# Last image's spectral filter: tokens stored twice side by side, one full-width first product instead of two half-width ones

## The chip, the cores and the metric

The kernel runs on one core of one Trainium2 chip, in one launch. A core has a matrix engine (TensorE, PE in the profile; its loads of the stationary operand are listed apart as PEld), VectorE (DVE), ScalarE (ACT), GpSimd (POOL), and a sync engine (SP), which here issues DMA transfers. The metric is device time in microseconds (us), before and after measured in alternation; less is better.

## The reference

Four images of 64x64 tokens with 96 channels pass through four layers. Layer 0 is a group norm with a selective scan in four directions, layer 1 a 3x3 convolution, layer 2 linear attention and a quantised feed-forward net. The change is in layer 3, which filters each hidden channel over all 4096 tokens in frequency:

```
t = t + filter(layer_norm(t)); t = t + ffn(layer_norm(t))

def filter(x):                                  # x: (B, 4096, 96)
    h = relu(bn1(einsum('bnc,hc->bnh', x, w1)))     # 192 hidden channels
    X = fft(h, axis=1, norm='ortho')                # over the tokens
    xr = relu(X.real * rd - X.imag * idg + rb)
    xi = relu(X.imag * rd + X.real * idg + ib)
    y = ifft(xr + 1j * xi, axis=1, norm='ortho').real
    return bn2(einsum('bnh,ch->bnc', y, w2))
```

`rd` and `idg` are the diagonals of two 192x192 matrices; bn1 and bn2 are normalisations with stored statistics.

## The kernel before

**Staging.** Images are b = 0 to 3. Channels lie on partitions and tokens along the free axis: `t` is 96 x 4096 f32, cut in 8 blocks (NBLK) of 512 tokens (BLK), each of 8 image rows (RPB). For most of the run VectorE, GpSimd and ScalarE do the scans of layer 0, and everything else is fed in as side lanes: generators that yield pieces with a price for each engine, and are advanced when a budget allows. What follows the scans of images 0 to 2 goes that way. The last image's has nothing to run beside; it is `tail`, which calls `rest(..., deep=2)` with 8 PSUM banks and two or four buffers where other images have one, and is drained one piece of each live stream in turn. The order on each engine is thus fixed when the program is built; each engine runs its own queue in that order.

**The last image's stages.** `rest` yields lists of streams. One list holds the convolution of layer 1 (products `p_l`, L953), the layer norm of the attention, the attention, the feed-forward net and two more layer norms; the last of these has the result name `ln_s` and feeds the filter. At the head of that list's set-up two tiles get a row of ones behind their 96 channels, so that a product with 97 rows adds a bias: `ln` (L1420) and `turned` (L1425), each by one GpSimd memset of 1x4096. In time this set-up stands in the feed-forward net of image 2 (`p_f`, L1166 and L1186; `y` and `z`, L877 to L890; `t`, L1196).

**The layer norm `ln_s`** (from L964) works in two halves of four blocks. Per block: the mean is taken off by a product (`p_mean`, L997), VectorE copies the result to `ln` (L988), ScalarE squares it (`sq`, L989), a product sums the squares (`p_var`, L979). Per half ScalarE and VectorE form 1/sqrt(variance) (L1018 to L1029), and a product spreads it over the channels (`p_rstd`, L1049). `scale` (L1033 on) multiplies: VectorE reads `ln` and `p_rstd` and writes into `turned` (L1040). `turned` is 97 x 4096 in the order (n2, n1), where token = 64 n1 + n2, so this write goes with a stride of 64 elements. ScalarE's queue has at this place also the shift of `t` (L1381).

**The filter.** The transform over 4096 points is done as 64 x 64. `filter_in` (L1208) makes three streams `third(hc)`, one for each 64 hidden channels. Each has eight banks k of eight columns j; for the column n2 = 8k+j it computes h for 64 tokens (n1) by a product with `turned[:, n2, :]` (97 x 64) stationary and `w1s[:, hs]` (97 x 64, bn1 folded in) moving:

```
for at in (0, N1):                                             # L1239
    nc.tensor.matmul(
        p[at : at + N1, j, :], lhsT=ln3[:, 8 * k + j, :], rhs=w1s[:, hs],
```

It does so twice, to partitions 0 to 63 and 64 to 127 of the PSUM bank `p_h`, for the gate (VectorE, L1224) takes max(p_h, 0) times `filt`, which holds `rd` on the first 64 partitions and `idg` on the others, and writes `hb`; after bank 0 the biases are added as an impulse (`imp`, L893). Then come eight banks of `p_dft` (L1262): each of 64 channels' `hb` (128 x 64, stationary) against the 64-point table for real and imaginary part (128 x 64 moving each), 16 products a bank, evacuated to `z` by ScalarE and VectorE in turn (L877, L881) and stored by SP (L1274). A stream starts its products when the one before has issued all its p_h and, with deep = 2, `hb` and `z` have a buffer free, so the streams overlap by a bank.

`filter_mid` then loads `zl` and the table `tw`, does the second transform (`p_dft2a` L1319, `p_dft2b` L1328), the relus and `p_o` with w2 (L1302, L1303); `filter_turn` (`p_idft`, L1368) and `filter_out` (`p_idft`, L1407) do the inverse transform; a last layer norm and feed-forward net end the program. `filter_out` leaves by VectorE (L1394).

An f32 product leaves two load records and two matmul records in the trace.

Of the kernel before, what the change touches and what calls it, by code (L numbers as in the profile page):

```python
# [10 lines left out]
F32 = mybir.dt.float32  # L11
# [9 lines left out]
L = HW * HW  # L21
C = 96
# [6 lines left out]
RPB = BLK // HW  # L29
HID = 384  # L30
N1 = 64
# [42 lines left out]
def layers(ctx: ExitStack, tc: tile.TileContext, a: dict, out):  # L74
# [4 lines left out]
    nc = tc.nc  # L79
# [132 lines left out]
    def settle(held):  # L212


        while held:
            cost, f, args, since = held[0]
            if cost[1]:
                while ordered[0] and clock[0] == since and (clock[0] - 1) % 8 in (7, 0, 1):
                    yield NEXT
            yield cost  # L220
            held.pop(0)
            f(*args)

    def until(ready):
        while not ready():
            yield NEXT
# [641 lines left out]
    def blk(i):  # L868
        return slice(i * BLK, (i + 1) * BLK)
# [25 lines left out]
    def rest(b, take, deep, x1t=None, held=None):  # L895
# [6 lines left out]
        def count(stage):  # L902
            return ready.get(stage, 0)
# [60 lines left out]
        def layernorm(wk, hold, dst, source, result, previous=None):  # L964

            def half_of(h):
                half = range(h * NBLK // 2, (h + 1) * NBLK // 2)
                yield from until(lambda: count(source) > half[-1 if source == "t1" else 0])  # L970
                yield from until(lambda: h == 0 or (result, "var", 0) in ready or deep > 1)
                pv, give_v = yield from take("p_var", 128)
                held, squares = [], []

                def variance():

                    i, sq = squares.pop(0)
                    at = 32 * (i - half[0])
                    nc.tensor.matmul(pv[at : at + 32, :], lhsT=mean_w, rhs=sq, start=True, stop=True)  # L979

                def centred(i, pm, give):
                    if squares and deep == 1:
                        variance()
                    sq = wk.tile([C, BLK], F32, tag=f"sq{h}", name="sq", bufs=1 if deep == 1 else 4)
                    if ordered[0]:
                        nc.scalar.copy(hold[:, blk(i)], pm)
                    else:
                        nc.vector.tensor_copy(hold[:, blk(i)], pm)  # L988
                    nc.scalar.activation(sq, pm, AF.Square)  # L989
                    give()  # L990
                    squares.append((i, sq))

                for i in half:
                    yield from until(lambda: count(source) > i)
                    pm, give = yield from take("p_mean", C, held=held)
                    yield (0.9, 0, 0, 0)
                    nc.tensor.matmul(pm, lhsT=centre, rhs=t[:, blk(i)], start=True, stop=True)  # L997
                    if squares and deep == 1:
                        yield (0.9, 0, 0, 0)
                        variance()  # L1000
                    yield from settle(held)
                    held.append(((0, 1.25, 0, 0), centred, (i, pm, give), clock[0]))
                while held or squares:
                    yield NEXT
                    if deep > 1:
                        yield from settle(held)
                    while squares:
                        yield (0.9, 0, 0, 0)
                        variance()
                    yield from settle(held)  # L1010


                yield from until(lambda: h == 0 or count(result) >= NBLK // 2)
                yield from until(lambda: previous is None or count(previous) == NBLK)
                y, w = (wk.tile([128, BLK], F32, tag=k, name=k, bufs=deep) for k in ("rs_y", "rs_w"))
                yield NEXT
                yield (0, 1.9, 0, 0)
                nc.scalar.activation(y, pv, AF.Ln, bias=num[:, 2:3])  # L1018
                nc.scalar.activation(y, y, AF.Exp, scale=-0.5)
                nc.scalar.activation(w, y, AF.Square)  # L1020
                yield NEXT
                yield (0, 0, 0, 0.7)
                nc.vector.scalar_tensor_tensor(w, pv, 1e-5, w, ALU.add, ALU.mult)
                give_v(True)
                ready[result, "var", h] = True
                yield NEXT
                yield (0, 0.65, 1.3, 0)
                nc.scalar.activation(w, w, AF.Identity, scale=-0.5, bias=num[:, 3:4])
                (nc.gpsimd if ordered[0] else nc.vector).tensor_tensor(y, y, w, ALU.mult)  # L1029
                yield NEXT  # L1030
                yield NEXT

                def scale(i, pr, give):  # L1033
                    kept = {} if dst.dtype == F32 else {"saturate": False}
                    to, x = dst[:, blk(i)], hold[:, blk(i)]
                    if result == "ln_s" and deep > 1:
                        to = turned[:C, :].rearrange("p (n2 n1) -> p n1 n2", n1=N1)
                        to = to[:, i * RPB : (i + 1) * RPB, :]
                        x, pr = (v.rearrange("p (n m) -> p n m", m=N1) for v in (x, pr))
                    nc.vector.tensor_tensor(to, x, pr, ALU.mult, **kept)  # L1040
                    give(True)
                    ready[result] = i + 1

                held = []
                for i in half:
                    pr, give = yield from take("p_rstd", C, held=held)
                    yield (1, 0, 0, 0)
                    at = slice(32 * (i - half[0]), 32 * (i - half[0]) + 32)
                    nc.tensor.matmul(pr, lhsT=pick[at, :], rhs=y[at, :], start=True, stop=True)  # L1049
                    yield from settle(held)  # L1050
                    held.append(((0, 0, 0, 0.7), scale, (i, pr, give), clock[0]))
                yield NEXT
                yield from settle(held)

            return [half_of(0), half_of(1)]
# [152 lines left out]
        def filter_in(wk, ln):  # L1208

            if deep > 1:  # L1210
                ln3 = turned.rearrange("p (n2 n1) -> p n2 n1", n1=N1)
            else:
                ln3 = ln.rearrange("p (n1 n2) -> p n2 n1", n2=N1)

            def third(hc):
                hs = slice(hc * N1, (hc + 1) * N1)
# [16 lines left out]
                for k in range(8):  # L1233
                    p, give = yield from take("p_h", 128, held=held)
                    p = p.rearrange("p (n h) -> p n h", h=N1)
                    for j in range(8):
                        if j % 4 == 0:
                            yield (1.3, 0, 0, 0)
                        for at in (0, N1):  # L1239
                            nc.tensor.matmul(  # L1240
                                p[at : at + N1, j, :], lhsT=ln3[:, 8 * k + j, :], rhs=w1s[:, hs],
                                start=True, stop=True,
                            )
                    yield from settle(held)
                    held.append(((0, 0, 0, 0.7), gate, (k, p, give), clock[0]))
# [9 lines left out]
                for k in range(8):  # L1255
                    p, give = yield from take("p_dft1", 128, held=held)
                    p = p.rearrange("p (h k) -> p h k", k=N1)
                    for j in range(8):
                        if j % 4 == 0:
                            yield (1.3, 0, 0, 0)  # L1260
                        for ri in range(2):
                            nc.tensor.matmul(  # L1262
                                p[ri * N1 : (ri + 1) * N1, j, :], lhsT=hb[:, 8 * k + j, :],
                                rhs=dft1[:, ri, :], start=True, stop=True,
# [13 lines left out]
            if deep > 1:  # L1278
                return [third(hc) for hc in range(3)]
            return [chain(*(third(hc) for hc in range(3)))]  # L1280

        def filter_mid(wk, os_):
# [135 lines left out]
        wk = normal.sbuf(f"ln{b}")  # L1418
        ln = wk.tile([C + 1, L], F32, tag="ln", name="ln")
        nc.gpsimd.memset(ln[C : C + 1, :], 1.0)  # L1420
        turned = None
        if deep > 1:

            turned = wk.tile([C + 1, L], F32, tag="turned", name="turned")
            nc.gpsimd.memset(turned[C : C + 1, :], 1.0)  # L1425
        mid = Region(tc)
        wk = mid.sbuf(f"mid{b}")
# [8 lines left out]
        ], [mid] + ([held] if held else [])  # L1436
        inner = Region(tc)
        yield filter_in(inner.sbuf(f"filter_in{b}"), ln), [inner, normal]
        wide, inner = Region(tc), Region(tc)
        os_ = wide.sbuf(f"os{b}").tile([128, C, N1], F32, tag="os", name="os")  # L1440
# [11 lines left out]
        wk = last.sbuf(f"last{b}")  # L1452
# [77 lines left out]
    while len(delta_places) <= N:  # L1530
        p = delta_places[-1]
# [208 lines left out]
    wk = weights.sbuf("weights", side="right")  # L1740
# [45 lines left out]
    wk = head.sbuf("pre0")  # L1786
# [14 lines left out]
    with tc.manual_schedule():  # L1801
        ordered[0] = True
        pas = [decay(0, 0, True), None, None, None]
        for n in range(N + 1):
# [51 lines left out]
            for k, q in enumerate(reversed(range(NCH))):  # L1856
# [26 lines left out]
                to = dls[n, 0] if alone else pas[q]  # L1883
# [153 lines left out]
```

## Time and profile before

| quantity | us |
|---|---|
| three runs, median | 5797.89 |
| three runs, lowest and highest | 5784.04, 5817.91 |
| profiled execution, its device time | 5791.5 |
| profiled execution, span of the core | 5789.7 |
| last image after the scans, `ln_s` to the end of the third p_dft | 5568 to 5638.8 |
| of that, first p_h to the last p_dft | 5587.70 to 5638.8 |
| busy over the span: TensorE, VectorE, GpSimd, ScalarE | 4187.2, 4858.5, 4417.0, 3020.1 |
| memset of the ones row of `turned` (L1425) | 3.51, at 5396.62 |
| VectorE into `turned` (L1040), each of 8 | 1.016 |

Times in the trace run from the span's start. A row of the timeline or of the groups gives the engine and line, the operation, out<-in by the program's names, the shape (for TensorE partitions*stationary columns, then the moving operand), the type and the number of records; what stands in brackets or behind the last bar is the time that the engine had been idle and what ended it. Shares over the whole span mix the scans with the last image's stages; the last image's filter is read from its own stretch. The mean granted TensorE clock of the run is 0.771 of full speed; in single windows it is 0.50 or 1.00.

### The profile page before, as it was taken

Reading aid. Unit: us, or ns where it says so; the run is one execution under the profiler, and the core shown is the slowest. Engines: PE = TensorE matmul, PEld = TensorE weight load, DVE = VectorE, ACT = ScalarE, POOL = GpSimd, SP = SyncE. Lnnn points to the kernel's source line nnn. Section 1 sums busy time; section 2 is a strip of 40 time slices with the busy share of each in tenths; the row PEclk is TensorE's granted clock in tenths of the full one; section 3 lists DMA queues with packets and bytes.
Section 4 is the critical chain, followed back from the end, with each engine's and each line's share of the span. In section 5 each row is a group of like instructions: output and inputs, shape, how many; then the busy total and the mean of one; then the engine's idle time right before and its main releaser. Section 6 shows DMA issues by size and latency. Waiting matters only on the chain. (4 is left out here: it accounts for less than half of the span.)

```text
span 5789.7 us, 65093 instructions
## 1 busy us (share of the span) xinstructions
PE 4187.2 (72%) x19818; PEld 1630.1 (28%) x19818; DVE 4858.5 (84%) x3610; ACT 3020.1 (52%) x4188; POOL 4417.0 (76%) x2148
## 2 busy tenths in 40 slices
PE   8978887778864777664477776667778667667878
PEld 4422222222211221241331221334222114323345
DVE  4188988888899898999799999999999999978364
ACT  4767766766663356545454446444544544434233
POOL 1378887888898778888788989888898898867200
PEclk9888898888866876666777886678678666777888
DMA  4378878876699878788988868679887678886013
GB/s 123 111 212 229 233 200 235 233 204 196 195 252 236 225 206 222 207 240 244 255 235 224 228 182 222 197 210 248 235 235 202 171 207 237 251 227 183 20 43 101
DMA packets 470107, 1174.80 MB, mean 203 GB/s; under 512 B 90768, under 2 KB 155900, under 8 KB 469628
## 3 DMA queue, kind: packets, MB, share of 16 engines
q1 hardware_dynamic: 469756, 1170.64, 74.1%
q8 instruction: 157, 2.57, 0.2%
q14 instruction: 194, 1.59, 0.1%
HBM read 1013.53 MB, written 156.76 MB: 202 GB/s over the span
## 5 line engine op out<-in xcount | busy, mean ns | idle before, releaser
L1574 POOL TENSOR_TENSOR S<-S,rep 128x1024 f32<-128x1024 f32 x768 | 1807.2, 2356 | 546.2 <-DVE S L1894 495.1
L1587 ACT ACTIVATE pa<-dl,nega 128x1024 f32<-128x1024 f32 x1152 | 1285.3, 1117 | 1431.9 <-DVE S L1894 1072.3
L1570 POOL TENSOR_TENSOR B<-B,rep 128x1024 f32<-128x1024 f32 x768 | 1798.0, 2355 | 119.0 <-DMA B<-du_s 70.8
L1833 DVE TENSOR_TENSOR_SCAN S<-pa,S,B 128x1024 f32<-128x1024 f32 x576 | 1352.3, 2348 | 315.6 <-ACT pa L1587 133.5
L1601 PE MATMUL py<-S,red 128*32 128x512 f32 x3072 | 908.5, 848 | 755.1 <-POOL S L1574 503.6
L1884 DVE TENSOR_TENSOR_SCAN pa<-pa,edge,B 128x1024 f32<-128x1024 f32 x438 | 1029.7, 2351 | 55.5 <-ACT pa L1587 55.5
L1894 DVE TENSOR_TENSOR S<-S,pa 128x1024 f32<-128x1024 f32 x630 | 763.6, 1212 | 1.9
L1833 DVE TENSOR_TENSOR_SCAN S<-pa,B 128x1024 f32<-128x1024 f32 x192 | 436.4, 2273 | 44.8 <-ACT pa L1587 35.8
L1601 PEld LDWEIGHTS py<-S,red 128*32 128x32 f32 x3072 | 110.0, 125 | 1232.7 <-POOL S L1574 728.3
L402 PE MATMUL p_conv<-low,conv_w 128*96 128x512 f32 x864 | 437.4, 658 | 14.1 <-ACT u L414 9.6
L1884 DVE TENSOR_TENSOR_SCAN pa<-pa,B 128x1024 f32<-128x1024 f32 x192 | 440.8, 2296 | 5.3
L154 ACT COPY side<-side 96x256 f32<-96x256 f32 (+1 forms) x448 | 279.0, 629 | 187.7 <-DMA deltaT_s<-side 79.9
L1884 DVE TENSOR_TENSOR_SCAN dl<-pa,edge,B 128x1024 f32<-128x1024 f32 x138 | 323.1, 2341 | 20.6 <-ACT pa L1587 16.6
L1175 POOL CAST h<-y 128x1536 fp8e5<-128x1536 f16 x64 | 95.5, 1492 | 303.2 <-ACT y L886 281.9
L1579 POOL TENSOR_TENSOR dl<-dl,rep 128x1024 f32<-128x1024 f32 x138 | 325.6, 2360 | 0.1
L402 PE MATMUL p_conv<-high,conv_w 64*96 64x512 f32 (+1 forms) x576 | 269.7, 605 | 0.0
L997 PE MATMUL p_mean<-t,centre 96*96 96x512 f32 x256 | 173.7, 791 | 99.0 <-ACT sq L989 48.4
L402 PEld LDWEIGHTS p_conv<-low,conv_w 128*96 128x96 f32 x864 | 149.5, 181 | 319.0 <-issue 289.8
L1601 PE MATMUL py<-dl,red 128*32 128x512 f32 x552 | 220.2, 717 | 21.1 <-POOL dl L1579 21.1
L1609 ACT COPY ys<-py 128x512 f32<-128x512 f32 x384 | 221.8, 578 | 19.5 <-PE py L1601 18.3
L647 PE MATMUL p_y<-side,ident 96*96 96x512 f32 x336 | 210.0, 774 | 28.1 <-DVE side L681 8.6
L953 PE MATMUL p_l<-x,taps 96*96 96x504 f32 (+3 forms) x432 | 199.4, 613 | 16.2 <-DMA x<-x 12.7
(245 smaller groups left out, 6024.0 us busy)
## 6 DMA issues: line engine op xcount, KB each, us to landing
dl<-delta_s SPq DMA_DIRECT2D x768, 256.0 KB
B<-du_s SPq DMA_DIRECT2D x768, 256.0 KB
B<-duT_s SPq DMA_DIRECT2D x768, 256.0 KB
dl<-deltaT_s SPq DMA_DIRECT2D x768, 256.0 KB
z_s<-z SPq DMA_DIRECT2D x48, 512.0 KB
zl<-z_s SPq DMA_DIRECT2D x64, 384.0 KB
side<-y_s SPq DMA_DIRECT2D x120, 192.0 KB
rep<-bc_s SPq DMA_DIRECT2D x64, 256.0 KB
```

Source lines behind the costliest of these rows:

```text
L154: nc.scalar.copy(o.rearrange("p (w h) -> p w h", h=HW), t[:n, :].rearrange("p (h w) -> p w h", w=HW)[:, q * w : (q + 1) * w, :],)
L402: nc.tensor.matmul(p, lhsT=conv_w[: src.shape[0], k, oc * C : (oc + 1) * C], rhs=src[:, ky : ky + RPB, kx : kx + HW], start=(k == 0), stop ...
L647: nc.tensor.matmul(p, lhsT=ident[:C, :C], rhs=x, start=(j == 0), stop=(j == 2))
L1570: nc.gpsimd.tensor_tensor(Bs[n, q], Bs[n, q], reps[n // NG, 0, q], ALU.mult)
L1574: nc.gpsimd.tensor_tensor(Ss[n, q], Ss[n, q], reps[n // NG, 1, q], ALU.mult)
L1579: nc.gpsimd.tensor_tensor(dls[n, 0], dls[n, 0], reps[n // NG, 1, 0], ALU.mult)
L1587: nc.scalar.activation(pa, dls[n, q], AF.Exp, scale=nega[:, g : g + 1])
L1601: nc.tensor.matmul(py[32 * j : 32 * j + 32, :], lhsT=red, rhs=x[:, k * BLK : (k + 1) * BLK], start=(i == 0), stop=(i == len(terms) - 1),)
L1609: nc.scalar.copy(ys, pys.pop((n, half)))
L1833: nc.vector.tensor_tensor_scan(s, pas[q], Bs[n, q], Ss[n, q - 1][:, CH - 1 : CH] if q else 0.0, ALU.mult, ALU.add,)
L1884: nc.vector.tensor_tensor_scan(to[:, ::-1], pas[q][:, ::-1], Bs[n, q][:, ::-1], edge if k else 0.0, ALU.mult, ALU.add,)
L1894: nc.vector.tensor_tensor(Ss[n, q], Ss[n, q], to, ALU.add)
```

## The change

It applies only where `deep` is over 1, which is the last image. `turned` becomes 97 x 8192 in the order (n2, k, n1) with k = 0, 1: each column's 64 tokens stand twice side by side. VectorE writes the copy k = 0 as before, with a stride of 128 elements; a new ScalarE copy for each block (L1042 of the changed kernel) reads it and writes k = 1. The ones row is memset over 1x8192. The stationary operand of p_h is now 97 x 128, and one product writes all 128 partitions, so that the three streams have 192 products of p_h instead of 384. The values are the same. The lines after L1042 move down by two to five (gate L1224 to L1226, p_h L1240 to L1242, p_dft L1262 to L1266).

```diff
@@ -1034,10 +1034,12 @@
                     if result == "ln_s" and deep > 1:
-                        to = turned[:C, :].rearrange("p (n2 n1) -> p n1 n2", n1=N1)
-                        to = to[:, i * RPB : (i + 1) * RPB, :]
+                        both = turned[:C, :].rearrange("p (n2 k n1) -> p k n1 n2", k=2, n1=N1)
+                        to, again = (both[:, k, i * RPB : (i + 1) * RPB, :] for k in range(2))
                         x, pr = (v.rearrange("p (n m) -> p n m", m=N1) for v in (x, pr))
                     nc.vector.tensor_tensor(to, x, pr, ALU.mult, **kept)
+                    if result == "ln_s" and deep > 1:
+                        nc.scalar.copy(again, to)
                     give(True)
@@ -1208,7 +1210,7 @@
             if deep > 1:
-                ln3 = turned.rearrange("p (n2 n1) -> p n2 n1", n1=N1)
+                ln3 = turned.rearrange("p (n2 m) -> p n2 m", m=2 * N1)
@@ -1236,9 +1238,11 @@
-                        for at in (0, N1):
+                        for at in (0, N1) if turned is None else (0,):
                             nc.tensor.matmul(
-                                p[at : at + N1, j, :], lhsT=ln3[:, 8 * k + j, :], rhs=w1s[:, hs],
+                                p[at : at + N1, j, :] if turned is None else p[:, j, :],
+                                lhsT=ln3[:, 8 * k + j, :],
+                                rhs=w1s[:, hs],
                                 start=True, stop=True,
                             )
@@ -1421,7 +1425,8 @@
-            turned = wk.tile([C + 1, L], F32, tag="turned", name="turned")
+            turned = wk.tile([C + 1, 2 * L], F32, tag="turned", name="turned")
             nc.gpsimd.memset(turned[C : C + 1, :], 1.0)
```

In each engine's queue the order is otherwise kept. TensorE does the eight banks of p_h for hc 0 and one of hc 1, then p_dft for hc 0; seven banks of hc 1 and one of hc 2, then p_dft for hc 1; seven banks, then p_dft for hc 2. In ScalarE's queue the first four copies stand ahead of two L1381, each followed by a sq L989, and of the rstd chain of the second half, the last four ahead of the evacuations of p_dft.

## The prediction

> **What bounds the kernel now.** I read the core's line first (5789.7 us, mean granted TensorE clock 0.771), then the groups, shape by shape, for the stretch after the scans (5480 to 5790 us), because everything that the diff touches belongs to the last image's filter. In these rows out<-in is followed by partitions*columns of the stationary operand and the shape of the moving one.
>
> ```profile
> L1240 PE MATMUL p_h<-w1s,turned 97*64 97x64 f32 x768 | 26.1, 236 | 4.2 <-DVE turned L1040 3.6 <-issue 0.6
> L1302 PE MATMUL p_o<-w2a,ya 128*128 128x96 f32 x128 | 25.9, 284 | 0.0
> L1240 PEld LDWEIGHTS p_h<-w1s,turned 97*64 97x64 f32 x768 | 25.6, 151 | 6.0 <-DVE turned L1040 5.3 <-issue 0.7
> ...
> L1224 DVE SCALAR_TENSOR_TENSOR hb<-p_h,filt 128x512 f32<-128x512 f32 x24 | 23.0, 1061 | 3.3 <-PE p_h L1240 3.3
> ...
> L1407 PE MATMUL p_idft<-os,vs 128*96 128x64 f32 x128 | 11.1, 248 | 0.8 <-issue 0.8
> ```
>
> Then the timeline of that stretch, which says what ends each wait:
>
> ```profile
> 5584.05 3.60 DVE L1040 TENSOR_TENSOR turned<-ln,p_rstd 96x512 f32<-96x512 f32 x4 [2.17 <-PE p_rstd L1049]
> 5587.70 11.22 PE L1240 MATMUL p_h<-w1s,turned 97*64 97x64 f32 x282 [3.65 <-DVE turned L1040]
> ...
> 5599.26 7.68 PE L1262 MATMUL p_dft<-dft,hb 128*64 128x64 f32 x256 [0.34 <-DVE hb L1224]
> ...
> 5606.77 6.94 PE L1240 MATMUL p_h<-w1s,turned 97*64 97x64 f32 x231
> ...
> 5614.27 0.97 PE L1240 MATMUL p_h<-w1s,turned 97*64 97x64 f32 x25 [0.56 <-issue]
> 5615.24 7.68 PE L1262 MATMUL p_dft<-dft,hb 128*64 128x64 f32 x256
> ```
>
> From 5587.70 to the end of the third p_dft near 5638.8 TensorE is hardly ever idle: **51.0 us, bound by TensorE**, with the VectorE gate (0.94 to 0.95 us a bank, back to back) close behind. Of that, one bank of p_h is 32 records (every f32 product leaves two matmul and two load records). Warm, 231 records in 6.77 us are 29.3 ns a record, 0.94 us a bank: two records, one for each half of the columns, every 58.7 ns. Before the clock comes up a record costs 53.3, a bank 1.70.
>
> **What one full-width product costs** is not in the p_h rows. The nearest rows in shape are p_o (128 stationary columns) and L1407 (96), both one after the other:
>
> ```profile
> 5654.13 0.39 PE L1302 MATMUL p_o<-w2a,ya 128*128 128x96 f32 x2
> 5654.35 0.39 PE L1303 MATMUL p_o<-w2b,yb 128*128 128x96 f32 x2
> 5654.57 0.39 PE L1302 MATMUL p_o<-w2a,ya 128*128 128x96 f32 x2
> ...
> 5184.60 0.64 PE L1303 MATMUL p_o<-w2b,yb 128*128 128x96 f32 x2
> 5185.03 0.63 PE L1302 MATMUL p_o<-w2a,ya 128*128 128x96 f32 x2
> ...
> 5282.05 6.66 PE L1407 MATMUL p_idft<-os,vs 128*96 128x64 f32 x40
> ```
>
> Two p_o records take 0.22 us warm (111 each) and 0.43 cold (213 each); L1407 takes 85 warm (160 cold) with 64 moving columns and 96 stationary ones. L1407 moves the same 64 columns as p_h and p_dft, whose two tiles together take 58.7, and still needs 85; p_gram, with 97 stationary columns, 86. So the **stationary columns** set the pitch: about columns/1.2 + 5, which is 58 for 64, 85 for 96 and 112 for 128, and twice that cold.
>
> **The Trainium skill** agrees where it can be held against the trace. "TensorE: Matmul & The Clock Gate", section LDWEIGHTS: a load costs about its column count over 1.2, in ns, whatever the rows; that gives 107 and 80 against 111 and 85 seen, so loads and products overlap and the longer of the two, the load, sets the pitch. The same page, Part 3: tiles of the array work at once; the two p_h halves start 7 ns apart here. Its Part 1: half clock is the default, and a window of some 3.4 us with enough activity releases it. Here the window view gives
>
> ```profile
> 5283.10:5286.50 3.40, 3.40 (x24) 3.40 (x23) 3.40 (x3) 0.98 (x1) 3.40 (x3) 0.50 0.69 212
> ...
> 5590.00:5594.00 4.00, 4.00 (x85) 4.00 (x84) 2.97 (x4) 0.00 (x0) 0.00 (x0) 0.53 0.00 0
> 5594.00:5600.00 6.00, 5.66 (x192) 5.53 (x188) 4.95 (x6) 0.00 (x0) 0.00 (x0) 1.00 0.02 5
> ```
>
> (length; busy PE, PEld, VectorE, ScalarE, GpSimd; clock). The first row is wholly L1407, loads back to back, and the clock stayed at 0.50 after it; dense p_h brought full clock at 5593.74. The page also has N columns pass in N/2.4 ns warm, twice that cold; with the two passes of a record, moving columns flow for 107 of each 160 ns of L1407, 0.67, and all the time in dense p_h. I counted this share over all windows of the trace: of some 350 cold ones below 0.65 none was followed by a warm one, of those above 0.95 93%. "SBUF — State Buffer", section Who interferes with whom: a VectorE operation in a two-port mode is blocked until GpSimd's ends. The trace agrees:
>
> ```profile
> 5396.62 3.51 POOL L1425 MEMSET turned<- 1x4096 f32 x1
> ...
> 5396.72 3.56 DVE L890 TENSOR_SCALAR z<-z,b_L 96x512 f16<-96x512 f16 x1
> ...
> 5400.90 0.72 ACT L886 ACTIVATE y<-y,b_L 128x512 f16<-128x512 f16 x1 [2.60 <-DVE y L881]
> ```
>
> That L890 otherwise takes about 0.35 (5403.52).
>
> **The change, part by part** (against the profiled span).
> 1. *Memset of the ones row, 1x4096 to 1x8192.* One partition, so twice as long: 3.51 to 7.0. It blocks VectorE, and with it ScalarE, p_f and GpSimd's own L1196 behind it; the chain runs on to z L881 at 5411.60, for which p_l L953 waits, and TensorE is dense from there. **+3.5** (0 if another gap takes it, 3.6 at most). The wider tile costs no transfer.
> 2. *Eight ScalarE copies, 96x512.* The nearest row is L154, a strided copy of 96x256, median 627 ns. 512 elements by its slope give about **1.05 us** (0.6 if stride cost nothing, like the 0.57 to 0.60 of L989; 1.5 at most). VectorE's L1040 stays at 1016 ns (its stride doubles; up to 0.2 more each). The first four wait for L1040 and stand ahead of L1381 and sq L989 in ScalarE's queue. The last product of L1040 ends near 5573.87, so the copy ends near 5575.0, where sq started at 5574.43 before; p_var, the rstd chain and p_rstd follow: **+1.2** (0.5 to 2.5). Of the last four three run under L1040; the last follows it and p_h waits for it now: 1.05 plus a hand-over of 0.3, **+1.4** (0.65 to 3.1). The z copies behind them come much later.
> 3. *p_h: 768 records of 64 columns become 384 of 128.* Half the records at the pitch of p_o: 16 by 111.5 = **1.78 us a bank warm, 3.41 cold**, against 0.94 and 1.70. The gates hide below it. The order on TensorE keeps p_h of hc 0 and one bank of hc 1 ahead of the first p_dft, so nine banks come at once. Moving columns flow for 107 of 213 ns in the cold state, 0.50: no window like that released the clock, so I take all nine cold: 9 x 3.41 = 30.7. The first p_dft (0.95 dense) then brings the clock up after one to two windows: 5.1 us of it cold (96 records), the other 160 records at 29.3: 9.8. Eight banks warm 14.3, p_dft 7.55, seven banks 12.5, wait for the last gate 1.45, p_dft 7.55, five changes between full-width and half-width products at about 0.2 (what p_o to p_dft2a shows) 1.0: together 85 against 51.0, **+34**. At the head p_h has nothing behind it on TensorE that could run meanwhile. Behind it zl and tw are loaded and TensorE waits 10.09 us for them; the stores of z come later with p_dft, so nothing absorbs the loss.
>
> Sum: 3.5 + 2.6 + 34 = **+40 us**: span 5830, that profiled execution's 5791.5 to 5831.5. The median, 5797.89, lies 6.4 higher; with it **5837**.
>
> **Rivals.**
> - *It warms all the same.* If two windows of full-width product suffice, as with p_h before, 6 us of the nine banks are cold (1.8 banks) and 7.2 run at 1.78, 18.9 for 30.7, and the first p_dft saves 2.3: the part is 71, +20; sum +26, 5824. For it: the array is as full as in old p_h. Against: L1407 and cold p_o windows (5184.1, share 0.71) stayed cold.
> - *It falls back to half clock in hc 1 and hc 2 too.* Warm, the share is 53/111.5 = 0.48. Warm windows of 0.45 to 0.50 stayed warm 60% of the time, of 0.35 to 0.45 half. With one window warm in each, eight banks take 24.2, seven 20.8, each p_dft 9.8: 108 for the part, sum +63, 5861. L1407's 0.62 stays warm, and full-width windows of 0.45 to 0.48 mostly did, so I take the warm one.
> - *Not slower: the loads hide.* If the load of the next 128 columns ran wholly under the current product, a record would cost 53 to 58 ns, a bank 0.94 as the gates, and clock would come as before. Then only points 1 and 2 are left, +6, or about nothing if the memset is absorbed: 5798 to 5804. For it: half as many instructions, and no pairs to keep in step. Against: p_o, which runs at its load. It decides below about 94 ns a record warm, at which the sum is 29 us, 0.5%. A gain has no room: the gates would take over at 0.94.
> - *The change does nothing* can't be: one product per column block writes all partitions.
>
> **How the numbers follow.** Central case 0.48, warms early 0.14, falls back 0.22, loads hide 0.13, something else 0.03. I predict the first. The before runs spread by 0.3% either way, so a difference of medians carries some 12 us. Loads hidden and the low end of early warming make the low end, falling back the high end: 5806 to 5868 (the central case alone 5822 to 5852). About 0.5% (29 us) is what a measurement can tell from no change. The central case falls within it 1 time in 5, early warming 2 in 3, hidden loads nearly always: same 0.31, faster 0.02, slower 0.67.
>
> **What would show it.** Memset near 7.0 us with an L890 of the same length beside it; eight ScalarE copies near 1.05, and p_h starting 2 to 3 us later after the memset's delay is taken off; p_h records 213 ns apart in the first nine banks at clock 0.50, 111 apart after; gates waiting for p_h in every bank; the three p_dft at 7.6 but for the first, near 10. I am wrong if p_h records come 55 to 60 ns apart, if the clock rises inside the first nine banks, or if it falls in hc 1.

## The result and the profile after

The changed kernel takes 5856.09 us (median of 4 runs, 5846.63 to 5865.7) against 5793.13 for the kernel before, run in turn with it (5784.04 to 5817.91): a ratio of **1.0098, 95% interval 1.0079 to 1.0117**, slower by 46 to 68 us. The profiled execution has a span of 5856.7 us, 67.0 above the one shown of before.

The timeline of the last image's filter in the changed kernel (start, length, engine, line, operation; in brackets the idle time before it and what ended it), with the rows that answer to those of the prediction:

```profile
5579.80 2.75 DVE L1040 TENSOR_TENSOR turned<-ln,p_rstd 96x512 f32<-96x512 f32 x3
...
5580.85 3.64 ACT L1042 COPY turned<-turned 96x512 f32<-96x512 f32 x3 [0.15 <-DVE turned L1040]
...
5595.07 3.60 DVE L1040 TENSOR_TENSOR turned<-ln,p_rstd 96x512 f32<-96x512 f32 x4 [2.17 <-PE p_rstd L1051]
5596.12 4.77 ACT L1042 COPY turned<-turned 96x512 f32<-96x512 f32 x4 [3.94 <-DVE turned L1040]
5600.94 30.98 PE L1242 MATMUL p_h<-w1s,turned 97*128 97x64 f32 x144 [5.85 <-ACT turned L1042]
...
5631.85 9.85 PE L1266 MATMUL p_dft<-dft,hb 128*64 128x64 f32 x256
...
5641.62 22.80 PE L1242 MATMUL p_h<-w1s,turned 97*128 97x64 f32 x128
...
5664.35 9.04 PE L1266 MATMUL p_dft<-dft,hb 128*64 128x64 f32 x256
...
5673.32 20.28 PE L1242 MATMUL p_h<-w1s,turned 97*128 97x64 f32 x112
...
5694.71 9.20 PE L1266 MATMUL p_dft<-dft,hb 128*64 128x64 f32 x256 [1.11 <-DVE hb L1226]
```

From the first p_h to the end of the last p_dft it is now **102.97 us instead of 51.15**. The groups of the same stretch say that TensorE is busy with p_h nearly three times as long with half the products (74.1 us instead of 26.1), and that the gates wait 52.9 us for it where they waited 3.3:

```profile
L1242 PE MATMUL p_h<-w1s,turned 97*128 97x64 f32 x384 | 74.1, 389 | 5.9 <-ACT turned L1042 5.9
L1242 PEld LDWEIGHTS p_h<-w1s,turned 97*128 97x128 f32 x384 | 73.5, 301 | 7.6 <-ACT turned L1042 7.5
L1226 DVE SCALAR_TENSOR_TENSOR hb<-p_h,filt 128x512 f32<-128x512 f32 x24 | 24.8, 1033 | 52.9 <-PE p_h L1242 52.9
```

And the windows (length; busy time and records of PE, PEld, VectorE, ScalarE, GpSimd; clock; transfers): nine banks at half clock, one stretch at full clock behind p_dft, and half clock again.

```profile
5601.50:5631.50 30.00, 30.00 (x143) 30.00 (x142) 8.50 (x9) 0.00 (x0) 0.00 (x0) 0.50 0.00 1
5642.00:5646.70 4.70, 4.70 (x45) 4.70 (x44) 2.52 (x3) 0.00 (x0) 0.00 (x0) 1.00 0.73 291
5646.88:5664.30 17.42, 17.42 (x83) 17.35 (x82) 5.13 (x5) 0.00 (x0) 0.00 (x0) 0.50 0.10 39
```

The 67.0 us by stretches, each between the same two instructions of the two traces:

| stretch | before | after | difference |
|---|---|---|---|
| start to the L890 ahead of the memsets (scans; no edit) | 5371.11 | 5376.19 | +5.1 |
| to the first p_l (memset of the ones row) | 41.23 | 44.72 | +3.5 |
| to the first L1040 of `ln_s` | 157.31 | 157.41 | +0.1 |
| to the first p_h (ScalarE copies) | 18.05 | 22.62 | +4.6 |
| to the end of the last p_dft (products) | 51.15 | 102.97 | +51.8 |
| to the end | 150.85 | 152.8 | +1.9 |

The first line belongs to no edit: it lies ahead of all of them, and single executions of one kernel differ by more (5784.04 to 5817.91 us). The last is a balance of both signs, mostly of the clock: it is at half speed for 10.24 us behind the last p_dft in both, but p_dft2a starts 2.8 us before the end of that in the kernel before, 4.6 in the changed one, which costs 0.7 up to p_idft L1368; and the changed kernel's clock fell at 5797.07, just as the p_mean of the last layer norm began, which costs 3.4. Later pieces are shorter and give 2.1 back. What the edits did adds up to 60 in this execution, within the interval of the ratio.

### The profile page after: what moved, and what is told of

Its sections match the earlier page's. It is cut to its first block, busy times and chain, and to the rows that moved or that the text cites. A ratio compares the mean times of both kernels' runs of the same rounds, so it can differ in the third digit from the quotient of the medians.

```text
span 5856.7 us, 64339 instructions
## 1 busy us (share of the span) xinstructions
PE 4245.5 (72%) x19434; PEld 1682.9 (29%) x19434; DVE 4863.6 (83%) x3610; ACT 3028.4 (52%) x4196; POOL 4421.4 (75%) x2148
## 5 line engine op out<-in xcount | busy, mean ns | idle before, releaser
L997 PE MATMUL p_mean<-t,centre 96*96 96x512 f32 x256 | 177.0, 804 | 98.2 <-ACT sq L989 47.3
L1614 ACT COPY ys<-py 128x512 f32<-128x512 f32 x384 | 221.9, 578 | 19.5 <-PE py L1606 18.9
```

Of the source, the lines that this page charges most:

```text
L1614: nc.scalar.copy(ys, pys.pop((n, half)))
```

## The experiments

In the diffs of this section `...` stands for code left out. The last image alone is changed in each.

**The product alone undone.** Everything of the change stays, but p_h is made by two half-width products again, each from its own copy of the tokens.

```diff
-    for at in (0, N1) if turned is None else (0,):
-        nc.tensor.matmul(p[:, j, :], lhsT=ln3[:, 8 * k + j, :], rhs=w1s[:, hs], ...)
+    for at in (0, N1):
+        two = slice(0, N1) if turned is None else slice(at, at + N1)
+        nc.tensor.matmul(p[at : at + N1, j, :], lhsT=ln3[:, 8 * k + j, two], rhs=w1s[:, hs], ...)
```

> Changed kernel with everything kept (tokens twice, eight ScalarE copies, the longer memset), but p_h made again by two half-width products, each with its own copy of the 64 tokens as stationary operand. Theory (the stationary load of 128 columns per product sets the pitch, and the thin flow of moving columns keeps the clock down): p_h records go back to about 58.7 ns a pair, the clock comes up within 7 us of the first p_h, and first p_h to last p_dft takes 50 to 54 us against 103; the run ends 48 to 53 us before the changed kernel and 6 to 12 us after the kernel before (memset 3.4, copies 4 to 5). Rival (the copies' and memset's wait, or the wider row pitch of the tile, slows the stage): p_h to p_dft stays above 65.

The ratio to before is 1.0008 (0.9994 to 1.0022). First p_h to last p_dft takes 52.98 us. Timeline:

```profile
5616.03 1.54 PE L1243 MATMUL p_h<-w1s,turned 97*64 97x64 f32 x12 [3.64 <-DVE turned L1040]
5618.28 10.62 PE L1243 MATMUL p_h<-w1s,turned 97*64 97x64 f32 x270 [0.71 <-ACT turned L1042]
5629.33 7.68 PE L1265 MATMUL p_dft<-dft,hb 128*64 128x64 f32 x256 [0.43 <-DVE hb L1226]
```

All that the products cost is gone; copies and memset stay. TensorE starts the lower half early and stops after 12 records for the copy of the last block. The copies' and the memset's 8 us can't be told from nothing by the medians, only in the trace.

**The product alone.** The kernel before with one full-width product for a column, and neither copies nor the longer memset.

```diff
+    n = min(8 * k + j, N1 - 2) * N1
+    one = turned[:, n : n + 2 * N1]
-    for at in (0, N1):
-        nc.tensor.matmul(p[at : at + N1, j, :], lhsT=ln3[:, 8 * k + j, :], rhs=w1s[:, hs], ...)
+    nc.tensor.matmul(p[:, j, :], lhsT=one, rhs=w1s[:, hs], ...)
```

> Kernel before with no second copy of the tokens and the short memset, but one full-width product per column, whose 128 stationary columns are the 64 tokens of this column and of the next one; so the upper half of h is computed from the wrong tokens, and the last column is read one early. Theory: layer norm and memset as before, p_h 213 ns a record cold and 111 warm, clock 0.50 through the first nine banks; first p_h to last p_dft 95 to 108 us, and the run 44 to 58 us slower than before, 5 to 10 us faster than the changed kernel. Rival (the copies set what is lost): as fast as before within 10 us.

The ratio to before is 1.0066 (1.0043 to 1.0088), slower by 25 to 51 us. In the profiled execution first p_h to last p_dft is 103.80 us, 52.7 more than before, while the stretch from the L890 ahead of the memsets to the first p_l (41.20) is unchanged. Timeline, p_h alone:

```profile
5582.14 30.98 PE L1244 MATMUL p_h<-w1s,turned 97*128 97x64 f32 x144 [3.64 <-DVE turned L1040]
...
5622.11 23.60 PE L1244 MATMUL p_h<-w1s,turned 97*128 97x64 f32 x128
```

So the loss is the full-width product's, whatever brings the tokens there. It is the same 30.98 for the nine banks as in the changed kernel. The medians show less than this execution's stage (38 us, at most 51) and less than the 44 to 58 expected of the run.

**More work for the same loads.** The changed kernel with the moving operand doubled.

```diff
-    nc.tensor.matmul(p[:, j, :], lhsT=ln3[:, 8 * k + j, :], rhs=w1s[:, hs], ...)
+    two = 2 if j < 7 else 1
+    nc.tensor.matmul(p[:, j : j + two, :], lhsT=ln3[:, 8 * k + j, :],
+                     rhs=w1s[:, hs].unsqueeze(1).broadcast_to([C + 1, two, N1]), ...)
```

> Changed kernel, with the moving operand of p_h doubled: each of the first seven products of a bank moves w1s twice, 128 columns, into its own 64 PSUM columns and the next 64, which the next product overwrites. The result is the same; TensorE gets nearly twice the moving columns for the same loads. Theory (load and product overlap, the load sets the pitch, the clock follows the flow of moving columns): p_h records stay at 107 to 114 ns warm, the clock is up at most 7 us after the first p_h and stays up through all three streams; first p_h to last p_dft 68 to 76 us against 103, so the run is 27 to 36 us faster than the changed kernel although it does more work. Rival A (the clock follows something that the extra columns don't change, the loads or the count of products): no change, 100 to 106 us. Rival B (load and product run one after the other): 160 ns warm or 320 cold, slower than the changed kernel by 30 us or more.

The ratio to before is 1.0055 (1.0037 to 1.0073). First p_h to last p_dft takes 83.18 us: neither the 68 to 76 of the theory nor the 100 to 106 of rival A. Windows of p_h in hc 0 and in hc 1:

```profile
5595.50:5622.80 27.30, 27.30 (x129) 27.18 (x128) 8.56 (x9) 0.00 (x0) 0.00 (x0) 0.50 0.00 1
5632.02:5646.58 14.56, 14.55 (x132) 14.36 (x128) 9.24 (x10) 0.00 (x0) 0.00 (x0) 1.00 0.37 145
```

Two parts of the theory held. The pitch is set by the load, and load and product overlap: 128 records in 14.56 us are 114 ns each warm, with an estimated 107 of moving columns under 107 of load (one after the other would be 213). The shares of time in which moving columns flow, here and below, are estimates of this kind and not records of the trace. They rest on the records that move 512 f32 columns: p_mean (L997) has one every 429 ns at full clock and every 853 at half clock, so 64 columns flow for 53 and 107 ns; two half-width products that run side by side count once. And p_h stays at full clock in hc 1 and hc 2, so with more work the stage is 20 us shorter. The third part did not hold: at half clock, with columns flowing for 0.937 of the time, the first nine banks never got the clock up. Is it the share, or the full width?

**The missing sixteenth.** All eight products of a bank move 128 columns, against half-width pairs thinned to the same 0.94.

```diff
 # from the run before: all eight move 128
-    two = 2 if j < 7 else 1
-    out_ = p[:, j : j + two, :]
+    out_ = p[:, min(j, 6) : min(j, 6) + 2, :]
 # from the kernel before: pairs, one column in sixteen in two parts of 32
+    cut = deep > 1 and j == 7 and k % 2 == 0
+    for part in (slice(0, 32), slice(32, N1)) if cut else (slice(0, N1),):
         for at in (0, N1):
-            nc.tensor.matmul(p[at : at + N1, j, :], lhsT=ln3[:, 8 * k + j, :], rhs=w1s[:, hs], ...)
+            nc.tensor.matmul(p[at : at + N1, j, part], lhsT=ln3[:, 8 * k + j, :], rhs=w1s[:, hs][:, part], ...)
```

> As the run with the doubled moving operand, but all eight products of a bank move 128 columns, the last one into its own 64 PSUM columns and those of the product before, so that one column in eight of h is replaced by its neighbour's (the result is off there). Moving columns then flow for 213 of each 213 to 218 ns cold, 0.98 of the time, where it was 0.937. Theory F (the clock is released by flow alone, from a share between 0.94 and 1.0): clock 1.00 at most 7 us after the first p_h; first p_h to last p_dft 71 to 77 us against 83.2. Theory W (full-width products with a load each don't release the clock, whatever their flow): clock 0.50 through all nine banks, 82 to 87 us.

> Kernel before, with its half-width pairs, but one column in sixteen is done by two pairs that move 32 columns each; the result is the same. For 17 loads a side there is then the flow of 16, 0.94 of the time, as in the run with the doubled moving operand, at half width. Theory F (flow alone, with the threshold above 0.94): the clock stays at 0.50 through the first nine banks, which take about 16.3 us, and the first p_dft loses 2; first p_h to last p_dft 57 to 61 us. Theory W (it is the full width that keeps it down): the clock is up at most 7 us after the first p_h, as before; 52 to 55 us.

With all eight at 128, first p_h to last p_dft takes 70.64 us (71 to 77 were expected), and the ratio to before is 1.0041 (1.0028 to 1.0053). The windows at the first p_h (at 5582.83):

```profile
5584.60:5588.03 3.43, 3.43 (x18) 3.43 (x18) 1.32 (x2) 0.00 (x0) 0.00 (x0) 0.50 0.00 0
5588.03:5591.40 3.37, 3.37 (x32) 3.37 (x31) 1.49 (x2) 0.00 (x0) 0.00 (x0) 1.00 0.00 0
```

One full window, and the clock is up. The thinned pairs, in the windows behind their first p_h (at 5574.55):

```profile
5577.24:5580.65 3.41, 3.41 (x70) 3.41 (x68) 2.16 (x4) 0.00 (x0) 0.00 (x0) 0.50 0.00 0
5580.65:5584.06 3.41, 3.41 (x70) 3.41 (x68) 1.90 (x3) 0.00 (x0) 0.00 (x0) 0.50 0.02 5
5584.06:5587.47 3.41, 3.41 (x70) 3.41 (x68) 2.01 (x2) 0.00 (x0) 0.00 (x0) 0.50 0.00 0
5587.47:5590.88 3.41, 3.41 (x68) 3.41 (x68) 2.11 (x2) 0.00 (x0) 0.00 (x0) 0.51 0.02 5
```

They stay at 0.50 through their nine banks (16.26 us), where untouched pairs needed 6.0 us. The last of these windows holds no thinned column and already the first records of p_dft (from 5590.50); its share is 0.99, and the clock came up behind it. So the first p_dft lost nothing, and first p_h to last p_dft is 56.51, between the ranges of the two theories. What decides is the clock: it did in both kernels what theory F says and in neither what theory W says. For p_h the width is no matter, the share of time in which moving columns flow is. (The thinned pairs ran once, so no verdict is read from their time.)

**The same thinness at half width.** The kernel before, each product in two parts of 32 columns.

```diff
-    for at in (0, N1):
-        nc.tensor.matmul(p[at : at + N1, j, :], lhsT=ln3[:, 8 * k + j, :], rhs=w1s[:, hs], ...)
+    for part in (slice(0, N1),) if deep == 1 else (slice(0, 32), slice(32, N1)):
+        for at in (0, N1):
+            nc.tensor.matmul(p[at : at + N1, j, part], lhsT=ln3[:, 8 * k + j, :], rhs=w1s[:, hs][:, part], ...)
```

> Kernel before (half-width pairs, no copies, short memset), but each product of p_h cut in two that move 32 columns each, so that every load of 64 stationary columns serves half as many moving ones; the result is the same. Theory (what matters is moving columns per load): a pair of records still takes about 58.7 ns warm and 107 cold, so a bank takes 1.88 and 3.41 us as in the changed kernel; moving columns flow for less than half of the time, the clock stays at 0.50 through the first nine banks and falls back in hc 1 and hc 2; first p_h to last p_dft 95 to 108 us, the run 44 to 57 us slower than before. Rival (the full width itself costs, through lost tiling or a changed mode, and half-width loads hide): below 65 us, the run within 15 us of before.

The ratio to before is 1.0073 (1.0055 to 1.0092), slower by 32 to 53 us where 44 to 57 were expected; first p_h to last p_dft takes 100.03 us. The windows in hc 0 and in hc 1:

```profile
5601.00:5628.00 27.00, 27.00 (x511) 27.00 (x510) 8.37 (x9) 0.00 (x0) 0.00 (x0) 0.50 0.01 2
5647.22:5659.00 11.78, 11.78 (x228) 11.78 (x225) 4.19 (x4) 0.00 (x0) 0.00 (x0) 0.50 0.01 3
```

This kernel has no full-width product, no copy and no longer memset, and it loses 49 of the changed kernel's 52 us in this stage. What the change did to TensorE was to halve the moving columns that each unit of loading time serves.

**The ones rows.** The kernel before, both rows of the last image loaded by a transfer.

```diff
-    nc.gpsimd.memset(ln[C : C + 1, :], 1.0)
+    nc.sync.dma_start(ln[C : C + 1, :], a["ones"])   # the last image alone
 ...
-    nc.gpsimd.memset(turned[C : C + 1, :], 1.0)
+    nc.sync.dma_start(turned[C : C + 1, :], a["ones"])
```

> Kernel before, with both rows of ones of the last image (in ln and in turned) loaded by a transfer from a constant instead of a GpSimd memset of 1x4096 each; the result is the same. Theory (the memset of turned is paid in full, since VectorE stands still under it and TensorE is dense behind it): no VectorE operation of 3.5 us in the feed-forward net of image 2, and what lies between the place of the first memset and the first p_l is 3 to 7 us shorter; the run 3 to 7 us (0.05 to 0.12 per cent) faster, which the medians can hardly tell. Rival (something else ends last there): no shorter.

The ratio to before is 0.9999 (0.9987 to 1.0012). From the L890 ahead of the memsets to the first p_l it is 38.93 us instead of 41.23: 2.3 shorter, not 3 to 7. In its timeline the stand-still is gone, but an L888 now takes 1.97 (0.35 to 1.25 in this stretch of the kernel before) and p_f waits 2.03 for VectorE:

```profile
5397.42 1.97 DVE L888 TENSOR_SCALAR y<-y,b_L 128x512 f16<-128x512 f16 x1
...
5400.04 0.59 PE L1166 MATMUL p_f<-q,w_L 96*128 96x512 fp8e5 x1 [2.03 <-DVE y L881]
```

So the 3.5 us for which a memset holds VectorE is not all to be had by taking it away. GpSimd's L1175 runs beside the long L888 (1.46 us from 5397.78); that this is what holds it wasn't tried. Nor did the 2.3 us reach the filter in this execution: from the first p_l to the first L1040 of `ln_s` it took 160.87 instead of 157.31.

## Why the prediction was right or wrong

The measured time lies inside the range, and it is slower, which had 0.67. But the likeliest case was not the one that came: its own range, 5822 to 5852, leaves out the measured 5856.09. What came was the second rival, the fall back to half clock in hc 1 and hc 2 (chance 0.22, 108 us for the part, sum +63), and the number fits only because the range left room for that rival: luck, as far as the likeliest case goes. (The sum of the likeliest case, 40 on 5797.89, is 5838, not 5837.) Step by step:

| step | predicted, us | measured, us |
|---|---|---|
| memset doubled | +3.5 | +3.5 |
| copies, first and second half together | +2.6 (1.1 to 5.6) | +4.6 |
| nine banks of p_h | 30.7 | 30.91 |
| p_dft of hc 0 | 9.8 | 9.77 |
| eight banks | 14.3 | 22.73 |
| p_dft of hc 1 | 7.55 | 8.97 |
| seven banks and the wait for the gate | 13.95 | 21.39 |
| p_dft of hc 2 | 7.55 | 9.20 |
| five changes between widths | 1.0 | in the rows above |

- **Memset.** 6.92 us, with an L890 of 6.97 beside it, and all of the added time on the path:

```profile
5401.77 6.92 POOL L1430 MEMSET turned<- 1x8192 f32 x1
...
5401.87 6.97 DVE L890 TENSOR_SCALAR z<-z,b_L 96x512 f16<-96x512 f16 x1
```

- **Copies: right mechanism, size off.** A copy takes 1.28 us, not 1.05, and four of them 4.77, while the four L1040 that feed them take 3.60. I counted only the last copy behind the last L1040; as the slower of the two the copies fell behind over each four, and the queue, L1385 and sq behind them, waited for that backlog too.
- **Pitch: right.** 3.41 us a bank of 16 records cold, 213 each (gates at 5608.06 and 5611.47), 1.78 warm (gates at 5643.66 and 5645.44). That the load sets it and that load and product overlap was read from p_o and L1407; the doubled moving operand shows it. "Not slower: the loads hide" fell with that.
- **Nine banks cold: right, and for the reason given.** The count of cold windows had no release below a share of 0.65, and p_h was at 0.50. (With the shares reckoned as here, 89 of 100 windows above 0.95 were followed by a warm one, not 93%.) The Trainium skill, "TensorE: Matmul & The Clock Gate", Part 1, has a window of 3.4 us with TensorE busy release the clock; here TensorE was busy in every one of these windows, loads and all, and with p_h it happened in this stretch only from a share of moving columns between 0.955 and 0.98. "It warms all the same" fell.
- **"I take the warm one": wrong.** The step was that at a share of 0.48 the clock holds in hc 1 and hc 2. It fell behind the first window that held only p_h, both times (at 5646.88 and 5677.60). That costs 8.4 and 7.4 us in p_h and 1.4 and 1.7 in the p_dft behind it, 18.9 together; the part exceeds its 85 by 18.1, since the 1.0 for changes between widths is in the rows. The step rested on pooled windows of all kinds and on a few full-width ones of other lines. The nearer rows stood in the same trace: eight warm windows that hold nothing but L1240 and a share of 0.42 to 0.48, in images 0 to 2, and half clock after each of the eight. One of them, at 0.48, and the window behind it:

```profile
3747.12:3750.52 3.40, 3.40 (x49) 3.40 (x50) 3.37 (x4) 0.54 (x1) 3.40 (x3) 1.00 0.75 257
3750.54:3753.94 3.40, 3.40 (x51) 3.40 (x49) 3.37 (x4) 0.95 (x2) 2.61 (x2) 0.50 0.75 204
```

  The share alone was my measure, pooled over products of other row counts than the 97 of p_h; I should have asked it of the rows of the same operation (what the row count has to do with it stands in the last section).
- **Not in the sum:** 1.9 us after the last p_dft, the balance given with the table of stretches.

## What to carry to other kernels

A product with a fresh stationary operand costs the longer of its load and its moving columns, so widening the stationary side at the same moving side makes an operation slower once the load is the longer; half as many instructions is no gain by itself. Two half-width tiles side by side fill the same array with half the load time. And when products run behind their loads, price the clock with them: below the share that holds it, every neighbour on TensorE pays as well (here 1.4 and 1.7 us in two p_dft).

## What the runs showed of the hardware that was not expected

Release and hold of the TensorE clock lie far apart. With p_h, from half clock, windows of the last image's filter at a share of 0.937 to 0.955 did not release it (seven full ones in a row with full-width products, three with pairs), one at 0.98 or more did. At full clock 0.89 held it in every window of two streams of p_h, L1407's 0.63 held it in the kernel before, the 0.48 of p_h did not. So extra moving columns that do nothing took 32 us off the changed kernel's stage (102.97 to 70.64): all of it by the clock, none by the pitch. In the trace of the kernel before, three windows of p_h alone at 0.50 to 0.61 kept it too, so for p_h the hold seems to end near a half; no run here was made to place it.

These lines are those of p_h, whose products have 97 rows. p_dft has 128, and its windows released the clock at smaller shares. In the kernel before, one that holds nothing but 56 records of p_dft, flowing for 0.87 of it, was enough:

```profile
3846.11:3849.52 3.41, 2.97 (x56) 2.97 (x58) 3.11 (x3) 1.19 (x2) 3.41 (x2) 0.50 0.68 211
3849.53:3852.93 3.40, 3.40 (x62) 1.88 (x60) 3.37 (x2) 0.60 (x1) 3.22 (x2) 1.00 0.14 48
```

The clock changes in these traces only on a grid of 3.41 us. Counted over the windows of that grid in all nine traces, the share fits much better when it is multiplied by the rows of the product over 128. Of 7052 windows at half clock, the best single line through the bare share (0.89) has 970 on the wrong side, the best line through the weighted one (0.745) 185; of 8191 at full clock it is 424 (0.435) against 97 (0.36). By this estimate dense p_h comes to 0.758, just above the line of release. The share of 0.937 comes to 0.71, below it, and the 0.48 that did not hold comes to 0.36, on the line of the hold. The count goes over products that differ in more than their rows, and no run here changed the rows alone, so that the rows are the cause is not shown.
